# A four-layer graph network on one core: the first layer's first weight as seven half-size products between those of its third weight, and larger stated times for the eigenvectors' operations

## The chip, the cores and the metric

The kernel runs on one core of a Trainium2 chip. The metric is the device time of one execution in microseconds (us), as the median of several runs; the runs before are 2282.12, 2283.62 and 2285.63 us. The profile is of one further execution.

## What is computed

The reference is a chain of four graph layers on x of 128 x 64 x 256 numbers (64 nodes in each of 128 graphs, 256 features), all in float32, with a layer norm of the sum of input and output after each. Only the first layer, and what runs beside it, is touched:

```python
def layer0(x, adj, W1, W2, W3):           # W1 256x512, W2 512x1024, W3 1024x256
    def conv(x, W):
        return einsum('nm,bmh->bnh', adj * adj, einsum('bnf,fh->bnh', x, W))
    h = relu(conv(x, W1))
    h = relu(conv(h, W2))
    return conv(h, W3)
x = layernorm(x + layer0(x, adj, W1, W2, W3))
```

The second layer needs U, the eigenvectors of a 64 x 64 normalised Laplacian that is made from adj. It doesn't depend on x, so the kernel computes it beside the first layer. The second layer is relu(U^T x W1 + b1) W2 + b2, multiplied by U; the third has four small recurrences over windows; the fourth is attention.

## The kernel before, in words

**Groups and stages.** The 8192 rows of x form 64 tiles of 128 rows. The first layer takes them in 16 groups of 4 tiles (loop over `g` in `layer0`, L1136). For a group, `burst` (L1046) multiplies by the squared adjacency in 64 x 64 quadrants, from rows or from `h1`, and ScalarE copies the result from PSUM into `m1` or `m2` (L1058). `weigh` (L1111) multiplies `m1` by the first weight `aw1`: for each of 4 tiles two matmuls of 128x512, and a relu into `h1`. The second weight takes `m2` to `h2`, the third `h2` to `s3`, and `mix_rows` (L1116) multiplies by the adjacency once more and adds the input.

**Seven products.** The second and the third weight are computed as 2 x 2 block products by a scheme with seven products instead of eight (`seven`, L1079): sums of blocks of the weight are made once (`sums_of_weights`, L1026; `signed_sums`, L1032), sums of blocks of the data per group. For the second weight `sums_second` (L1129) makes these on VectorE. For the third they go into the tile `sh` by DMAs that add into their destination: `adds` (L1043) issues these from POOL's queue (L1044), and `less` (L1040) prepares negated blocks on ScalarE. Product 5 of the third weight reads slot 0 of `sh`, product 6 slot 1, product 7 slot 2 and product 3 slot 3. Products accumulate in PSUM banks: each chain holds one bank with the tag `ch` (two buffers), one `ps` (three buffers, shared with the bursts) and one `b5` (two buffers), by `bank` (L1023). Results are evicted by copies on ScalarE (L1096 to L1098), adds on VectorE, and where the result is an activation, a relu on ScalarE (L981) after the add.

**What sets the order.** This part of the kernel is scheduled by hand: the order of the Python code is the order on each engine. `seven` is a generator that emits one product at each step; `layer0` interleaves two chains for the second weight and then advances the chain `w3` of the third weight, with the four `weigh` between products 2 and 5 and the bursts for the next group between its later products. The eviction of a product is put off: `step` (L1014) emits the one before after the next product has been emitted.

**The eigenvectors beside it.** `eigen` (L275) is a generator, too: a Householder reduction of 62 steps, each with a 128x128 matmul into `pa` (L312), some 24 small VectorE operations and a square root on ScalarE (L397); then six passes of a bisection, a recurrence D2, and the vectors. `between` (L961), called after each matmul of the first layer, advances it when its time has come on a clock `now` that counts stated TensorE time. `Timed` (L42) wraps VectorE: each operation it emits moves the clock `free` on by a stated time `least` plus 0.0009 us for each element beyond 64. `V.least` is 0.21 us, in the bisection 0.278; `VL`, with 0.25, wraps the first layer's own VectorE operations. All operations through `Timed` carry L52 in the profile, all matmuls of the weights L972. The remaining layers are ordered by a planner (`Plan`) that the change doesn't touch; its instructions carry L162.

Of the kernel before, what the change touches and what calls it, by code (L numbers as in the profile page):

```python
# [11 lines left out]
F32 = mybir.dt.float32  # L12
# [29 lines left out]
class Timed:  # L42
# [1 line left out]


    def __init__(self, engine, free, until):
        self.engine, self.free, self.until, self.least = engine, free, until, 0.21

    def __getattr__(self, name):
        def give(out, *args, **kw):  # L50
# [224 lines left out]
def eigen(tc, stack, a, ident, cst, u2, ut2, now, free):  # L275
# [10 lines left out]
    until = [0.0]  # L286
    V, S, PE = Timed(nc.vector, free, until), nc.scalar, nc.tensor
# [5 lines left out]
    def sb(shape, tag):  # L293
        uid[0] += 1
        return wp.tile(shape, F32, tag=tag, name=f"{tag}_{uid[0]}")
# [9 lines left out]
    def soon():  # L305
        return max(free[0], until[0]) - 0.45
# [75 lines left out]
    for i in range(N - 2):  # L382
# [3 lines left out]
        q = sb([N, 16], "q")  # L386
# [67 lines left out]
    d, e, ep, g = (de[:, j:j + 1] for j in range(4))  # L454
# [40 lines left out]
    w = cp.tile([N, 20, N], F32, name="w")  # L495
# [66 lines left out]
    for _ in range(PASSES):  # L562
        V.tensor_scalar(h2, h2, 1.0 / (FAN + 1), None, op0=ALU.mult)
        x = sb([W, FAN], "bx")
# [4 lines left out]
        for k in range(1, HALF):  # L569
            r = sb([W, FAN], "br")  # L570
# [3 lines left out]
        r = sb([W, FAN], "br")  # L574
# [28 lines left out]
    for k in range(1, N):  # L603
        c = N - 1 - k
        t = sb([W, 1], "tw")
        V.reciprocal(t, D2[:, c + 1:c + 2])
        V.tensor_scalar(D2[:, c:c + 1], t, es2[:, k:k + 1], dl[:, k:k + 1], op0=ALU.mult, op1=ALU.add)
        yield soon()
    V.least = 0.21
    D = cp.tile([N, 2, N], F32, name="D")  # L610
    for k in range(2):
        V.tensor_scalar(D[:, k, :], D2[k * N:(k + 1) * N, :], 1e15, -1e15, op0=ALU.min, op1=ALU.max)
# [149 lines left out]
P = 128  # L762
# [74 lines left out]
def kernel(  # L837
# [26 lines left out]
    V, S, PE = nc.vector, nc.scalar, nc.tensor  # L864
# [14 lines left out]
    wa = phase_a.enter_context(tc.tile_pool(name="wa", bufs=1))  # L879
    pa = phase_a.enter_context(tc.tile_pool(name="pa", bufs=1))  # L880
# [3 lines left out]
    def load(pool, name, src, pattern, shape, **kw):  # L884
        t = pool.tile(shape, F32, name=name)
        nc.sync.dma_start(t, src.rearrange(pattern, **kw))
        return t
# [6 lines left out]
    order = list(range(RING, NT // 4)) + list(range(RING))  # L894

    def rows_of(g):

        return X[:, 4 * g:4 * g + 4, :] if g < RING else XA[:, 4 * (g - RING):4 * (g - RING) + 4, :]
# [11 lines left out]
    aw1 = load(wa, "aw1", a_w1, "(k p) f -> p k f", [P, 2, 512], p=P)  # L910
# [72 lines left out]
    def quads(c):  # L983
        for m in (slice(0, N), slice(N, P)):
            for h, hs in enumerate((slice(0, N), slice(N, P))):
                yield m, slice(c * P + m.start, c * P + m.stop), h, hs
# [5 lines left out]
    tv = wa.tile([P, 5, 4, P], F32, name="tv")  # L992
    m1 = pa.tile([P, 2, 512], F32, name="m1")
    h1 = pa.tile([P, 4, 512], F32, name="h1")
    m2 = pa.tile([P, 4, 512], F32, name="m2")
    ss = pa.tile([P, 3, 2, 256], F32, name="ss")
    h2 = pa.tile([P, 2, 8, 256], F32, name="h2")
    sh = pa.tile([P, 4, 4, 256], F32, name="sh")
    s3 = pa.tile([P, 4, D], F32, name="s3")
# [8 lines left out]
    free = [0.0]  # L1008
    VL = Timed(V, free, now)
# [13 lines left out]
    def bank(tag="ps"):  # L1023
        return tl(psa, [P, 512], tag, bufs={"ps": 3, "ch": 2, "b5": 2}[tag])

    def sums_of_weights(w, b12):  # L1026
        VL.tensor_sub(w[7], w[3], b12)
        VL.tensor_sub(w[5], b12, w[1])
        VL.tensor_sub(w[6], w[3], w[5])
        VL.tensor_sub(w[4], w[2], w[6])  # L1030

    def signed_sums():  # L1032
        w = third[0]
        VL.tensor_sub(w[7], D12, D22)
        VL.tensor_sub(w[5], D12, D11)
        VL.tensor_sub(w[6], D22, w[5])
        VL.tensor_sub(w[4], D21, w[6])
        VL.tensor_scalar(w[3], D22, -1.0, None, op0=ALU.mult)

    def less(slot, j, c):  # L1040
        S.activation(sh[:, slot, 2 * j:2 * j + 2], h2[:, 0, 4 * c + 2 * j:4 * c + 2 * j + 2, :], AF.Identity, scale=-1.0)

    def adds(out, src):  # L1043
        nc.gpsimd.dma_start(out, src, accum_op=ALU.add)  # L1044

    def burst(dst, src, c):  # L1046
        to = dst.rearrange("p c (t h n) -> p h c t n", h=2, n=N)
        p = [bank().rearrange("p (c t n) -> p c t n", c=2, t=4) for _ in range(2)]
        for t in range(4):
            for k in range(2):  # L1050
                for m, f, h, hs in quads(c + k):
                    PE.matmul(p[h][m, k, t, :], src[hs, t, f], sqT2[hs, hs], start=True, stop=True)  # L1052
        now[0] += QUADS
        between()

        def result():
            for h in range(2):
                S.copy(to[:, h, c:c + 2], p[h])  # L1058

        step(result)  # L1060

    def chained(out, pairs, new):
        for m, some in enumerate(pairs):
            for i, (lhsT, rhs) in enumerate(some):
                mm(out[:, m, :], lhsT, rhs, new and m == i == 0, i == len(some) - 1, skip_group_check=True)

    def by_second(j):

        def product(out, i, new):
            w, a = (x[i] for x in second)  # L1070
            chained(out, [[(w[:, k, c * P:(c + 1) * P], a[:, k, :]) for k in range(2)] for c in (2 * j, 2 * j + 1)], new)

        return product

    def by_third(out, i, new):
        w, a = (x[i] for x in third)
        chained(out, [[(a[:, k, r * P:(r + 1) * P], w[:, k, :]) for k in range(4)] for r in range(2)], new)

    def seven(n, product, c11, c12, c21, c22, last, order=(1, 2, 6, 5, 7, 3, 4)):  # L1079

        def view(b):
            return b[:, :2 * n].rearrange("p (i n) -> p i n", i=2)

        def add(dst, b):
            VL.tensor_add(dst, dst, b)
            if last is relu:
                relu(dst, dst)

        ch = view(bank("ch"))
        for i in order:  # L1090
            if i in (2, 5):
                b = view(bank("ps" if i == 2 else "b5"))
                b2, b5 = (b, None) if i == 2 else (b2, b)
            out = {2: b2 if i == 2 else None, 5: b5 if i == 5 else None, 3: b5 if i == 3 else None}.get(i, ch)
            product(out, i, i in (1, 2, 5))
            step({1: lambda: S.copy(c11, ch), 2: lambda: add(c11, b2), 6: lambda: S.copy(c12, ch),  # L1096
                  5: lambda: S.copy(c22, b5), 7: lambda: add(c22, ch), 3: lambda: add(c12, b5),
                  4: lambda: last(c21, ch)}[i])  # L1098
            yield i
# [11 lines left out]
    def weigh(t):  # L1111
        p = bank()
        run(p, [(m1[:, k, t * P:(t + 1) * P], aw1[:, k, :]) for k in range(2)])
        step(lambda: relu(h1[:, t, :], p))
# [21 lines left out]
    def layer0():  # L1136
        n = NT // 4
        burst(m1, rows_of(order[0]), 0)
        step()
        for t in range(4):  # L1140
            weigh(t)
            if t == 1:
                sums_of_weights(second[0], B12)
        step()
        for c in (0, 2):
            burst(m2, h1, c)
            step()
        for g in range(n):
            last = g == n - 1
            then = {} if last else {  # L1150
                (1, 1): lambda: less(2, 0, 0),
                (0, 5): lambda: (less(2, 1, 0), nc.sync.dma_start(sh[:, 1], sh[:, 2])),
                (1, 7): lambda: less(3, 0, 1),
                (0, 4): lambda: (nc.sync.dma_start(sh[:, 0], H22), adds(sh[:, 1], H22)),
                (1, 4): lambda: less(3, 1, 1),
            }
            sums_second()
            w2 = [seven(256, by_second(j), *[h2[:, r, 4 * c + 2 * j:4 * c + 2 * j + 2, :] for r in (0, 1) for c in (0, 1)],
                        relu) for j in range(2)]
            for j in (0, 0, 1, 0, 1, 0, 1, 0, 1, 0, 1, 0, 1, 1):  # L1160
                then.get((j, next(w2[j])), lambda: None)()
            if g == 0:
                signed_sums()
                burst(m1, rows_of(order[1]), 0)
            if last:
                for _ in plain():
                    pass
            else:
                q = [s3[:, r:r + 2, c:c + P] for r in (0, 2) for c in (0, P)]
                w3 = seven(P, by_third, *q, S.copy, order=(1, 2, 5, 6, 7, 3, 4))  # L1170
                next(w3)
                for slot in range(3):
                    adds(sh[:, slot], H21)
                adds(sh[:, 3], sh[:, 1])
                next(w3)
                for t in range(4):
                    weigh(t)
                next(w3)
                next(w3)
                burst(m2, h1, 0)  # L1180
                next(w3)
                next(w3)
                burst(m2, h1, 2)
                next(w3)
                if g + 2 < n:
                    burst(m1, rows_of(order[g + 2]), 0)
            for t in (0, 2):
                mix_rows(g, t)
        step()
# [71 lines left out]
    V, S, G, Q = (Noted(plan, e) for e in ("DVE", "ACT", "POOL", "SP"))  # L1261
# [585 lines left out]
```

## Time and profile before

| what | before |
|---|---|
| median of three runs | 2283.62 us |
| the profiled execution | 2283.95 us, its span 2282.0 us |
| first layer, from the start to the first matmul after it | 0 to 838.3 us |
| eigenvectors, last matmul | 689.6 us |
| TensorE matmul records, busy | 2236.5 us, 98% of the span |
| VectorE busy | 1710.0 us, 75% |
| ScalarE busy | 1217.1 us, 53% |
| granted TensorE clock | 0.995 |

The profile names the engines PE (TensorE matmuls), PEld (its weight loads), DVE (VectorE), ACT (ScalarE), POOL and SP. A line of the timeline gives the start, the length of the stretch, the engine, the source line, the operation with the tiles it writes and reads, the shape and how many records; a number in brackets is the engine's idle time just before, with what ended it. A float32 matmul leaves two records. Tiles are named without their numbers: `ps<-aw,m` is the first weight by `m1`, `ch<-aw,h` the first product of the third weight, `b<-tv,sh` its products 5 and 3, and `ps<-sqT,h` a burst. A line of busy times by stretch gives the stretch, its length, the busy time of each engine, the granted clock, the DMA engines' share and GB/s.

### The profile page before, as it was taken

What the parts mean: (1) busy time and instruction counts of PE and PEld (TensorE: products, weight loads), DVE (VectorE), ACT (ScalarE), POOL (GpSimd) and SP (SyncE); (2) the same over time, 40 slices, a digit from 0 to 9 for tenths busy, and PEclk for the clock granted to TensorE, in tenths of its full rate; (3) what the DMA queues carried; (4) which work ended last, traced back from release to release, by engine and by line L of the source; (5) the groups of instructions that cost most, each with busy time, mean ns of one, the idle gap of its engine ahead of it and who ended that gap; (6) DMA issues with size and microseconds to landing.
All of it is one profiled execution on the core that took longest, in us unless ns stands there. A gap on an engine that the chain in (4) does not pass through costs nothing.

```text
span 2282.0 us, 52665 instructions
## 1 busy us (share of the span) xinstructions
PE 2236.5 (98%) x20660; PEld 1993.6 (87%) x20660; DVE 1710.0 (75%) x5816; ACT 1217.1 (53%) x2954; POOL 204.1 (9%) x390
## 2 busy tenths in 40 slices
PE   7999999999999999999999999999999999999997
PEld 5877888888878888999999999999999999999985
DVE  5888888788881139766967977977877887578977
ACT  2444444454444445665655655655655656566554
POOL 0111111111111110000100000000010010000112
PEclk9999999999999999999999999999999999999998
DMA  8334333333443231000111211211221220001331
GB/s 267 74 89 90 87 77 75 75 82 77 108 93 79 66 125 57 11 10 20 66 38 50 77 57 50 86 57 40 87 66 40 78 72 32 31 29 64 110 115 49
DMA packets 95240, 163.01 MB, mean 71 GB/s; under 512 B 24976, under 2 KB 65936, under 8 KB 94992
## 3 DMA queue, kind: packets, MB, share of 16 engines
q1 hardware_dynamic: 83840, 120.05, 15.8%
q0 software_dynamic: 10800, 39.33, 9.1%
q8 instruction: 162, 2.65, 0.5%
q14 instruction: 86, 0.70, 0.1%
q10 hardware_dynamic: 352, 0.28, 0.0%
HBM read 57.64 MB, written 45.09 MB: 45 GB/s over the span
## 4 chain that ended last, share of the span: by engine, by line
PE 85%; DVE 10%; DMA 2%; issue 1%; ACT 1%; SPq 1%; POOL 1%; ACTq 0%; DVEq 0%; POOLq 0%
PE ps L162 57%; PE ch L972 12%; PE ps L972 9%; PE b L972 5%; PE ps L1052 2%; DVE q L52 1%; DVE w L162 1%; DMA XA<-in_x_dram 1%; DVE D L52 1%; DVE h L52 1%; DVE gates L162 1%; PE pa L312 1%; DVE X L162 1%; DVE xr L52 1%; DVE junk L52 1%
## 5 line engine op out<-in xcount | busy, mean ns | idle before, releaser
L162 PE MATMUL ps<-w,wih 128*128 128x128 f32 (+2 forms) x2944 | 572.0, 298 | 0.8 <-ACT gates L162 0.7
L162 PEld LDWEIGHTS ps<-w,wih 128*128 128x128 f32 x2944 | 453.1, 191 | 27.0 <-issue 6.5
L162 PE MATMUL ps<-w,sums 128*128 128x128 f32 (+2 forms) x3104 | 476.1, 293 | 0.0
L162 PEld LDWEIGHTS ps<-w,sums 128*128 128x128 f32 x3104 | 422.7, 191 | 13.9 <-ACT gates L162 1.6
L162 ACT ACTIVATE gates<-gates,cbi 128x256 f32<-128x256 f32 (+4 forms) x736 | 314.1, 479 | 172.0 <-DVE gates L162 170.1
L162 DVE TENSOR_TENSOR gates<-gates,ps 128x512 f32<-128x512 f32 (+4 forms) x408 | 233.9, 583 | 169.8 <-PE ps L162 156.8
L162 ACT COPY gates<-ps 128x512 f32<-128x512 f32 (+4 forms) x408 | 204.2, 506 | 252.0 <-PE ps L162 244.7
L162 PE MATMUL ps<-hs,whh 128*128 128x128 f32 (+1 forms) x896 | 181.2, 284 | 0.2 <-DVE hs L162 0.2
L162 PE MATMUL ps<-w,whh 128*128 128x128 f32 (+1 forms) x896 | 181.1, 284 | 0.0
L162 ACT ACTIVATE gates<-ps,cbi 128x128 f32<-128x128 f32 (+2 forms) x368 | 119.5, 385 | 43.3 <-PE ps L162 42.6
L162 POOL TENSOR_SCALAR rs<-mv 128x2 f32<-128x2 f32 x96 | 23.3, 253 | 1326.7 <-DVE mv L162 1325.4
L162 PEld LDWEIGHTS ps<-hs,whh 128*128 128x128 f32 x896 | 139.7, 191 | 0.3 <-DVE hs L162 0.3
L162 PEld LDWEIGHTS ps<-w,whh 128*128 128x128 f32 x896 | 139.8, 191 | 0.0
L981 ACT ACTIVATE h<-h 128x512 f32<-128x512 f32 x96 | 60.4, 630 | 147.7 <-DVE h L52 147.7
L972 PE MATMUL ch<-m,tw 128*128 128x256 f32 x512 | 123.3, 384 | 1.1 <-DVE h L52 0.8
L972 PE MATMUL ps<-aw,m 128*128 128x512 f32 x256 | 118.1, 607 | 1.2 <-ACT m L1058 1.2
L972 PE MATMUL b<-ss,aw 128*128 128x256 f32 x512 | 118.6, 379 | 0.0
L972 PEld LDWEIGHTS ch<-m,tw 128*128 128x128 f32 x512 | 96.7, 192 | 16.0 <-DVE h L52 3.5
L972 PEld LDWEIGHTS b<-ss,aw 128*128 128x128 f32 x512 | 97.2, 190 | 13.3
L972 PEld LDWEIGHTS ps<-aw,m 128*128 128x128 f32 x256 | 47.5, 194 | 50.8 <-issue 46.0
L162 PE MATMUL ps<-hs,sums 128*128 128x128 f32 (+1 forms) x448 | 90.6, 284 | 0.0
L162 ACT ACTIVATE gates<-c 128x256 f32<-128x256 f32 (+1 forms) x176 | 75.5, 432 | 27.4 <-DVE c L162 26.1
(369 smaller groups left out, 4150.4 us busy)
## 6 DMA issues: line engine op xcount, KB each, us to landing
sh<-h POOLq DMA_DIRECT2D x60, 512.0 KB, 6.5
far<-w SPq DMA_DIRECT2D x42, 512.0 KB, 2.8
w<-far SPq DMA_DIRECT2D x168, 128.0 KB, 3.0
X<-rest SPq DMA_DIRECT2D x24, 512.0 KB, 3.3
out_dram<-X SPq DMA_DIRECT2D x64, 128.0 KB, 1.8
sh<-sh SPq DMA_DIRECT2D x15, 512.0 KB, 2.9
sh<-h SPq DMA_DIRECT2D x15, 512.0 KB, 2.9
sh<-sh POOLq DMA_DIRECT2D x15, 512.0 KB, 4.9
```

The costliest lines, as they stand in the source:

```text
L52: return getattr(self.engine, name)(out, *args, **kw)
L162: getattr(e, name)(*[real(x) for x in args], **{k: real(v) for k, v in kw.items()})
L312: PE.matmul(out, lhsT, rhs, start=True, stop=True)
L972: PE.matmul(out, lhsT, rhs, start=start, stop=stop, **kw)
L981: S.activation(dst, src, AF.Relu)
L1052: PE.matmul(p[h][m, k, t, :], src[hs, t, f], sqT2[hs, hs], start=True, stop=True)
```

## The change

The first weight is made into seven products as well, from group 1 on (group 0 still uses `weigh`). A chain `w1` with a width of 256 is advanced between products of `w3`; its data sums are three VectorE operations on `m1` (`sums_first`), emitted while the group before its use is at the second weight, and a fourth (`X12`) after product 2. The order of the two chains' products is 3.1, 1.1, 3.2, 1.2, 1.6, 1.5, 3.5, 1.7, 1.3, 3.6, 1.4, where the digit before the point is the weight; then a burst for the upper half of `h1`'s columns, 3.7, a burst for the lower half, 3.3 and 3.4. Before, the lower half came first, after 3.6, and the upper after 3.3. The stated time of the eigenvectors' operations goes from 0.21 to 0.23 us; that of the bisection stays at 0.278.

```diff
-        self.engine, self.free, self.until, self.least = engine, free, until, 0.21
+        self.engine, self.free, self.until, self.least = engine, free, until, 0.23
...
-    V.least = 0.21
+    V.least = 0.23
...
+    W11, W12, W21, W22 = (aw1[:, r, c:c + 256] for r in (0, 1) for c in (0, 256))
+    tu = wa.tile([P, 3, 256], F32, name="tu")
+    X11, X12, X21, X22 = (m1[:, k, r:r + 256] for r in (0, 256) for k in (0, 1))
+    sx = pa.tile([P, 2, 256], F32, name="sx")
+    first = ((None, W11, W21, W22, tu[:, 2], W12, tu[:, 1], tu[:, 0]),
+             (None, X11, X12, X12, X22, sx[:, 0], sx[:, 1], X21))
...
+    def sums_first():
+        VL.tensor_add(sx[:, 0], X21, X22)
+        VL.tensor_sub(sx[:, 1], sx[:, 0], X11)
+        VL.tensor_sub(X21, X11, X21)
...
+    def by_first(out, i, new):
+        w, a = (x[i] for x in first)
+        chained(out, [[(a[:, r * P:(r + 1) * P], w)] for r in range(2)], new)
...
                 (1, 1): lambda: less(2, 0, 0),
+                (1, 6): lambda: sums_first() if g else None,
...
             if g == 0:
                 signed_sums()
+                sums_of_weights(first[0], W12)
                 burst(m1, rows_of(order[1]), 0)
...
-                q = [s3[:, r:r + 2, c:c + P] for r in (0, 2) for c in (0, P)]
-                w3 = seven(P, by_third, *q, S.copy, order=(1, 2, 5, 6, 7, 3, 4))
+                w3 = seven(P, by_third, *[s3[:, r:r + 2, c:c + P] for r in (0, 2) for c in (0, P)], S.copy,
+                           order=(1, 2, 5, 6, 7, 3, 4))
+                w1 = seven(256, by_first, *[h1[:, r:r + 2, c:c + 256] for r in (0, 2) for c in (0, 256)], relu)
                 next(w3)
                 for slot in range(3):
                     adds(sh[:, slot], H21)
                 adds(sh[:, 3], sh[:, 1])
+                if g == 0:
+                    sums_first()
+                next(w1)
                 next(w3)
-                for t in range(4):
-                    weigh(t)
-                next(w3)
+                next(w1)
+                VL.tensor_sub(X12, X12, sx[:, 1])
+                for w in (w1, w1, w3, w1, w1, w3, w1):
+                    next(w)
+                burst(m2, h1, 2)
                 next(w3)
                 burst(m2, h1, 0)
                 next(w3)
-                next(w3)
-                burst(m2, h1, 2)
                 next(w3)
```

## The prediction, made before the changed kernel had run

> **What bounds the kernel now.** I read the page's busy times first, then busy time by stretch, then TensorE's order of work in the stage that changes, then its waits, and last the engines that feed that stage.
>
> ```profile
> PE 2236.5 (98%) x20660; PEld 1993.6 (87%) x20660; DVE 1710.0 (75%) x5816; ACT 1217.1 (53%) x2954; POOL 204.1 (9%) x390
> ```
>
> TensorE bounds the whole. By stretch (PE, PEld, DVE, ACT, POOL busy us):
>
> ```profile
> 300.00:440.00 140.00, 139.63 (x1153) 114.24 (x1151) 114.62 (x651) 68.50 (x184) 19.73 (x33) 1.00 0.39 91
> 440.00:640.00 200.00, 200.00 (x1771) 166.38 (x1771) 174.58 (x651) 93.08 (x210) 27.28 (x44) 1.00 0.36 86
> 690.00:840.00 150.00, 149.50 (x1274) 125.74 (x1278) 29.14 (x49) 65.68 (x153) 16.26 (x30) 1.00 0.28 67
> ```
>
> Layer 0 lies at 0 to 838 us, and TensorE has hardly a gap in these stretches. VectorE is over 80% busy while the eigenvectors are computed (to 690 us), 19% after. A group without eigenvector work shows the stage that changes (start, length, records):
>
> ```profile
> 725.77 1.95 PE L972 MATMUL ch<-aw,h 128*128 128x128 f32 x16
> 727.55 1.95 PE L972 MATMUL ps<-aw,h 128*128 128x128 f32 x16
> 729.34 7.03 PE L972 MATMUL ps<-aw,m 128*128 128x512 f32 x16
> 736.21 1.95 PE L972 MATMUL b<-tv,sh 128*128 128x128 f32 x16
> ```
>
> From start to start, a product of the third weight takes 1.78 us and the first weight, plain, 6.87. Groups start every 49.12 us here (699.78, 748.90), every 51.7 to 53.1 in the Householder part. Where TensorE waits (in brackets):
>
> ```profile
> 47.45 0.46 PE L312 MATMUL pa<-AQ,LV 128*128 128x128 f32 x2 [3.44 <-DVE LV L52]
> 104.22 0.46 PE L312 MATMUL pa<-AQ,LV 128*128 128x128 f32 x2 [0.74 <-DVE LV L52]
> 161.81 1.99 PE L972 MATMUL ch<-m,tw 128*128 128x256 f32 x8 [0.35 <-DVE h L52]
> 643.56 2.05 PE L972 MATMUL ch<-tv,h 128*128 128x128 f32 x16 [0.93 <-DVE s L52]
> ```
>
> All such waits from 60 to 690 us come to 6.2 us: VectorE behind its stated times. Last, what stands behind a group's final products (third weight begins at 320.46 there):
>
> ```profile
> 320.93 0.67 DVE L52 TENSOR_TENSOR h<-h,b 128x512 f32<-128x512 f32 x1
> ```
>
> ```profile
> 321.63 0.63 ACT L981 ACTIVATE h<-h 128x512 f32<-128x512 f32 x1 [0.83 <-DVE h L52]
> 322.29 0.63 ACT L1041 ACTIVATE sh<-h 128x512 f32<-128x512 f32 x1
> 322.83 0.58 ACT L981 ACTIVATE h<-ch 128x512 f32<-128x512 f32 x1
> ```
>
> ```profile
> 319.69 0.92 POOL L1044 DMA_DIRECT2D sh<-h  x1 [4.56 <-ACT h L981]
> 323.77 0.86 POOL L1044 DMA_DIRECT2D sh<-h  x1 [3.17 <-ACT LV L385]
> ```
>
> The second weight's last add starts 0.47 us after the third's first product, and ScalarE reads the `ch` bank of its last product until 323.4, 2.95 us after it. In the group at 725.77 the same read ends 0.97 us after. Nobody needed this bank or these sums soon; the change makes two products need them.
>
> **What the Trainium skill says.** "Perfetto Trace Analysis", Identifying the Most-Contended Engine: matmul busy share is no measure of distance from the limit; look at weight loads. The trace agrees: matmul records overlap (379 ns long, 216 apart), so I price by starts. Same page, Matmuls: independent groups should rotate through PSUM banks, so that eviction overlaps; with two `ch` banks for four chains this is where I expect the cost. "VectorE: DVE Perf Modes", the TRN2 errata: an fp32 tensor_tensor takes (N+151)/0.96 ns, so 424 ns for 256 and 691 for 512 elements; the trace has 410 (`s<-s,ps`) and 674 (`h<-h,b`). "DMA: Bandwidth & Descriptors", Anatomy of one DMA: 2.0 us plus bytes at 436 GB/s, an estimate of 3.2 us for 512 KB; the accumulating ones here land after 4.6 (727.11) to 6.5 us (375.59), and I use these.
>
> **The change, part by part.** I call the start of the third weight's first product 0, its products 3.1 to 3.7, the first weight's 1.1 to 1.7.
>
> *TensorE work.* Removed in each of groups 0 to 14: 6.87 us. Added: 7 products of 2 matmuls, 4 records of 128x256 each; eight such records take 1.73 us (751 to 765), so 28 take 6.04. Saved 0.83 x 15 = **12.4 us**, on the path, since TensorE is busy throughout there.
>
> *VectorE and ScalarE work.* Per group VectorE gets four 128x256 operations (0.41) and three 128x512 adds (0.67): 3.7 us in 48, some 8%; it had 18% free. ScalarE had four evictions (2.4 us), now three copies, three relus and one eviction (4.2): hidden, it is half idle. `sums_first` stands seven products before it is needed. Group 0 pays 1.6 us of weight sums behind a backlog on VectorE; product 1.6 starts at 5.3, the sums are done some 3 us in: nothing, or 1 us if late. The 8% itself I cost at nothing, covered by the free share; with that gone it would be 3.7 us a group.
>
> *Stated times 0.21 to 0.23.* VectorE's real pitch is 0.212 (24 operations of a Householder step in 5.09 us from 329.33), more in early groups. With 0.23 it keeps pace, so most waits above go: of 2.4 us before `LV` some 1.7, of the 0.84 before `h` all, of the 3.44 at 47.45 about 1: **-3.5 us** (0 to -5). The eigenvectors end later: in the built order their last matmul moves into group 15, with 60 half-products of 0.43 us and 1.7 us behind it, 27 us. So the end stays covered; without that cover each us of delay counts in full.
>
> *Wait A: 1.1 for its bank.* It takes the bank of the second weight's last product, and stands at 1.78. ScalarE frees it 2.5 us after the last add starts. Following the built order of VectorE, ScalarE and the eigenvector matmuls, with these durations, over its five repeating phases the add starts at about -0.4, 0, -0.8, 0.2 and 0.7, which makes waits of 0.4, 0.7, 0, 0.9 and 1.2. Ten groups (0 to 9) have Householder steps, so 6.4; I take **5.9 us** (3 to 10), as later steps have shorter operations. In the groups with the bisection the POOL issue came at 1.34 to 2.0, hence the bank at 1.0 to 1.6: no wait.
>
> *Wait B: the burst right after 1.4.* It reads what 1.3 completes, through an add (0.67) and a relu (0.63), with 3.6 and 1.4 (2.64 us) as cover. In the same five phases 0, 0.3, 1.0, 0.5, 0, over nine groups: **3.2 us** (1 to 6). Queued behind the waiting matmuls is all of TensorE's order, including eigenvector matmuls.
>
> *Wait C: 3.5 for the accumulating DMA.* It moves from 10.4 (736.21) to 7.0. The DMA's issue at 1.34 lands at 5.9 without eigenvector work; in the other groups at 3.3, landing at 8.7 (323.77 and 5.4). Wait A itself delays 3.5 to 7.9 on average, with an eigenvector matmul 8.2. What remains: **1 us** (0 to 15). The later accumulates (3.6, 3.7, 3.3) have over 1 us to spare. POOL's and SP's queues keep their order; nothing passes them.
>
> *Group 14* now meets the D2 recurrence, where two operations take 0.505 us against a stated 0.46: 1 us (0 to 3).
>
> *After layer 0* the built order of TensorE is unchanged; only release waits of the later weights' loads differ, on tiles finished earlier: nothing. A load freed 1 us late could cost that 1 us; there is no gain in it, since the loads issued at 821 to 839 us land before VectorE's first sums of them (850.8).
>
> **Sum** against the profiled execution (2283.95 us, span 2282.0 and 1.95 around it): -12.4 - 3.5 + 5.9 + 3.2 + 1 + 1 = -4.8, so 2279.1. The median of the runs is 0.33 us lower: **2278.7**.
>
> **Rivals.** 0.2% (4.6 us) is about what a measurement can tell from no change.
> 1. *The waits hardly come.* A slower stated pace lets VectorE run ahead to its data, as in the bisection groups; A and B fall to some 2 us and C and group 14 to none: -12.4 - 3.5 + 2 = -13.9, 2269.7. For: bisection groups show no such delay. Against: the constant 3.3 us issue in five groups, set by ScalarE's square root in between.
> 2. *The waits take all.* A and B at their upper ends (16 us): -12.4 - 3.5 + 16 + 2 = +2, 2286; or, in the middle, 2283. For: both waits hang on three engines' queues in a row.
> 3. *Slower: C decides.* In the group at 372.21 the add was issued at 3.4 and landed at 9.9, 2.6 us after 3.5 would want it. If half of the ten groups are so, C is 13, A in the rest 3.5, B 3.2, group 14 1: -15.9 + 20.7 = +4.8, 2288.4. It decides once landings in the ten groups average beyond some 9.3. For: H22's add is in the same queue. Against: in the built order that add comes earlier.
>
> **Chances.** Forecast (gain of 3 to 9 us) 0.45, rival 1 0.20, rival 2 0.22, rival 3 0.13. Beyond 0.2% faster: rival 1 and 0.27 of the forecast, 0.47; slower: rival 3 and 0.02 of rival 2, 0.15; the rest, 0.38, the same. Range: 2270.5, leaving out a quarter of rival 1, to 2288.5, leaving out half of rival 3.
>
> **What would show it.** The first weight's 28 records in 6.0 us; groups 10 to 13 at about 48.3 us; waits before `ch<-aw,m` (A) near 0.6 us a group and before `ps<-sqT,h` (B) near 0.3, up to about 480 us; no wait on a DMA before `b<-tv,sh`. The forecast is wrong if C stands there regularly, if bisection groups wait too, or if the eigenvectors end after layer 0.

## The result and the profile after

The changed kernel takes 2281.1 us (median of 20 runs), the kernel before 2284.77 in the same comparison: a ratio of 0.9983, 95% interval 0.9976 to 0.9990, so 3.9 us faster (2.3 to 5.5). The profiled execution took 2280.57 us with a span of 2278.8; before, the span was 2282.0. The first matmul after the first layer starts at 834.10 (before 838.34), 4.2 us earlier. What follows takes 1444.7 us, before 1443.7; over the profiles of both kernels and of experiments 1 to 11 it scatters from 1442.0 to 1444.7, so that 1.0 us is not read as an effect. One place alone makes up more than that: four records of a later matmul, `ps<-w,dw`, take 3.65 us from 2186.02 at a granted clock of 0.79 (2184 to 2192), behind a wait of 2.43 us; before, they take 1.96 us at 1.00, behind a wait of 2.33 us.

Busy times of the whole, first part of the page after:

```profile
PE 2224.0 (98%) x20840; PEld 2026.2 (89%) x20840; DVE 1758.0 (77%) x5925; ACT 1239.0 (54%) x2999; POOL 205.2 (9%) x390
```

TensorE's busy time fell by 12.5 us, the span by 3.2. The difference, 9.3 us, is idle time of TensorE that was not there before. Busy time by stretch shows it (PE, PEld, DVE, ACT, POOL):

```profile
300.00:440.00 140.00, 137.37 (x1325) 122.54 (x1324) 110.17 (x575) 70.58 (x187) 18.62 (x30) 1.00 0.39 91
440.00:640.00 200.00, 198.04 (x1821) 174.83 (x1820) 162.35 (x681) 100.02 (x239) 26.60 (x44) 1.00 0.36 85
690.00:840.00 150.00, 145.21 (x1185) 125.40 (x1185) 103.30 (x387) 67.75 (x161) 17.60 (x33) 1.00 0.30 78
```

PE is idle for 2.6, 2.0 and 4.8 us in these stretches, where it was for 0.4, 0 and 0.5. VectorE's 103 us in the last stretch (before 29) are the eigenvectors, which now reach into groups 14 and 15; their last matmul is at 806.04, 28 us ahead of the end of the layer. The stage that changed, in a group where nothing waits here (start, length, records, the timeline of PE):

```profile
616.55 1.95 PE L972 MATMUL ch<-aw,h 128*128 128x128 f32 x16
618.33 1.03 PE L972 MATMUL ch<-aw,m 128*128 128x256 f32 x4
619.20 1.95 PE L972 MATMUL ps<-aw,h 128*128 128x128 f32 x16
620.98 1.03 PE L972 MATMUL ps<-aw,m 128*128 128x256 f32 x4
621.85 1.03 PE L972 MATMUL ch<-tu,sx 128*128 128x256 f32 x4
```

A product of the first weight takes 0.87 us from start to start (618.33 to 619.20, 620.98 to 621.85), seven of them 6.1 instead of 6.87. Group 11 is 48.76 us long (590.55 to 639.31), 0.38 of it a wait. The waits, from the timeline of PE (idle time before, with its releaser, in brackets):

```profile
49.36 0.77 PE L312 MATMUL pa<-AQ,LV 128*128 128x128 f32 x2 [4.33 <-DVE LV L52]
...
110.49 1.13 PE L972 MATMUL ch<-aw,m 128*128 128x256 f32 x4 [0.70 <-ACT h L981]
123.56 1.16 PE L1063 MATMUL ps<-sqT,h 64*64 64x64 f32 x64 [0.91 <-ACT h L981]
...
264.45 1.13 PE L972 MATMUL ch<-aw,m 128*128 128x256 f32 x4 [1.02 <-ACT h L981]
...
630.28 1.16 PE L1063 MATMUL ps<-sqT,h 64*64 64x64 f32 x64 [0.38 <-ACT h L981]
673.74 2.02 PE L972 MATMUL b<-tv,sh 128*128 128x128 f32 x16 [1.25 <-DMA sh<-h]
...
762.88 1.99 PE L972 MATMUL ch<-m,tw 128*128 128x256 f32 x8 [0.51 <-DVE h L52]
768.19 1.13 PE L972 MATMUL ch<-aw,m 128*128 128x256 f32 x4 [1.53 <-ACT h L981]
...
789.90 1.95 PE L972 MATMUL ps<-s,sqT 128*128 128x512 f32 x4 [1.08 <-DVE s L52]
```

`ch<-aw,m` behind ScalarE is wait A (product 1.1 for its bank), `ps<-sqT,h` wait B (the burst for the relu of 1.3), `b<-tv,sh` behind a DMA wait C. A comes in groups 1 to 7 and 9 with 0.70, 0.92, 0, 1.02, 0.93, 0.32 and 0.61, and 0.70; group 3 and, five groups on, group 8 have none: it repeats every five groups, and shrinks. These eight groups come to 5.2 us. B comes seven times with 0.22 to 0.91. Waits on `LV` are gone but for the first one, which has grown from 3.44 to 4.33. The last three lines shown, 3.1 us together, lie in group 14 and are counted there: D2's operations stand on VectorE from 724.1 to 764.2, so the first wait falls beside them and the other two behind them. The 1.53 is of A's kind; with it A is 6.7 us.

How A comes about, in group 1. VectorE:

```profile
107.85 0.69 DVE L52 TENSOR_TENSOR h<-h,b 128x512 f32<-128x512 f32 x1
```

and ScalarE:

```profile
108.57 0.63 ACT L981 ACTIVATE h<-h 128x512 f32<-128x512 f32 x1 [1.92 <-DVE h L52]
109.23 0.63 ACT L1052 ACTIVATE sh<-h 128x512 f32<-128x512 f32 x1
109.77 0.19 ACT L397 ACTIVATE q<-q 64x1 f32<-64x1 f32 x1
109.86 0.57 ACT L981 ACTIVATE h<-ch 128x512 f32<-128x512 f32 x1
```

The bank is read by the last line, which ends at 110.43; 1.1 starts at 110.49. Ahead of this relu stand the relu of the sum that VectorE made (108.57) and a negation for `sh` (`less`, L1052), which nobody needs yet at this point. Experiment 9 starts from here.

### The profile page after: what moved, and what is told of

It is laid out like the page before. It is cut to its first block, busy times and chain, and to the rows that moved or that the text cites. A ratio compares the mean times of both kernels' runs of the same rounds, so it can differ in the third digit from the quotient of the medians.

```text
span 2278.8 us, 53192 instructions
## 1 busy us (share of the span) xinstructions
PE 2224.0 (98%) x20840; PEld 2026.2 (89%) x20840; DVE 1758.0 (77%) x5925; ACT 1239.0 (54%) x2999; POOL 205.2 (9%) x390
## 4 chain that ended last, share of the span: by engine, by line
PE 83%; DVE 10%; DMA 2%; ACT 2%; issue 1%; SPq 1%; POOL 0%; ACTq 0%; DVEq 0%; POOLq 0%
PE ps L162 57%; PE ch L972 12%; PE b L972 6%; PE ps L972 5%; PE ps L1063 2%; DVE h L52 1%; DVE w L162 1%; DMA XA<-in_x_dram 1%; ACT h L981 1%; DVE D L52 1%; PE pa L312 1%; DVE X L162 1%; DVE gates L162 1%; DVE q L52 1%; DMA sh<-h 1%
## 5 line engine op out<-in xcount | busy, mean ns | idle before, releaser
L981 ACT ACTIVATE h<-h 128x512 f32<-128x512 f32 x141 | 89.0, 631 | 248.3 <-DVE h L52 248.2
L162 DVE TENSOR_TENSOR w<-w,w 128x128 f32<-128x128 f32 (+2 forms) x264 | 80.7, 316 | 8.1 <-PE ps L162 4.4
L162 DVE SCALAR_TENSOR_TENSOR c<-gates,c 128x256 f32<-128x256 f32 (+1 forms) x112 | 50.0, 446 | 41.1 <-ACT gates L162 40.8
```

The lines of the kernel that those rows point to most:

```text
L162: getattr(e, name)(*[real(x) for x in args], **{k: real(v) for k, v in kw.items()})
L981: S.activation(dst, src, AF.Relu)
```

## The experiments

The theory: the products save what they should, and the eigenvectors' small operations, in the order of VectorE and ScalarE, delay what 1.1, 3.5 and the burst wait for. The rivals: the products lose by themselves (banks, DMAs), and the stated time is what gains, or the other way round. All times are against the kernel before, run beside each kernel; the yardstick of the changed kernel is its 0.9983. A difference between two such ratios is uncertain by some 3 us (an estimate from the intervals of both). Against the changed kernel, experiments 1, 6 and 7 are slower and 10 and 11 faster beyond this; 5, 8, 9 and 12 lie about as far from it as this or nearer, so there the single waits in the traces carry the argument.

C counts every wait of 3.5 that ends within 0.15 us of the landing of its DMA. The profile puts some of these down to a VectorE instruction (`b<-tv,sh` at 321.89 in experiment 5, landing at 321.76).

**1. The seven products alone, with the old stated time.**

```diff
-        self.engine, self.free, self.until, self.least = engine, free, until, 0.23
+        self.engine, self.free, self.until, self.least = engine, free, until, 0.21
...
-    V.least = 0.23
+    V.least = 0.21
```

> The seven products alone, with the stated time left at 0.21. Theory (the seven products save 12.4 us of TensorE work and pay in waits for evictions that stand behind eigenvector operations on VectorE; the larger stated time takes VectorE out of arrears): the saving stays, the old waits before LV and h stay and the new ones grow, so 3 to 7 us slower than the changed kernel, about level with the kernel before. Rival (the larger stated time only moves the eigenvectors' end and buys nothing): level with the changed kernel, 4 us faster than before.

Measured: 2289.8 us against 2283.62, ratio 1.0029 (1.0018 to 1.0039): 6.2 us slower than before, some 10 slower than the changed kernel, more than expected. Two of its waits on PE:

```profile
113.97 1.13 PE L972 MATMUL ch<-aw,m 128*128 128x256 f32 x4 [2.60 <-ACT h L981]
...
161.69 0.46 PE L312 MATMUL pa<-AQ,LV 128*128 128x128 f32 x2 [0.72 <-DVE LV L52]
```

A adds up to 11.9 us (6.7 in the changed kernel with group 14), the waits on `LV` after the first to 2.5 (none), C to 2.3, B to 4.0, about what it was in the changed kernel. The layer ends at 844.77. So the seven products on their own lose. The reading that VectorE has more of the first layer's work, and is told to take the eigenvectors' operations faster than it can, fits these waits.

**2. The stated time alone**, in the kernel before.

```diff
-        self.engine, self.free, self.until, self.least = engine, free, until, 0.21
+        self.engine, self.free, self.until, self.least = engine, free, until, 0.23
...
-    V.least = 0.21
+    V.least = 0.23
```

> The kernel before with only the stated time of the eigenvectors' operations raised to 0.23, no seven products for the first weight. Theory: some of the 6.2 us of waits from 60 to 690 us go, 2 to 4 us faster than before. Rival (the whole gain of the change is the seven products' net): within 1 us of before.

Measured: 2282.46 against 2283.62, ratio 0.9993 (0.9985 to 1.0001): by the ratio 1.6 us, which the interval can't tell from nothing. The waits before `LV` that remain are 0.17 to 0.33, but the wait of 3.4 that was 0.93 is 2.71, one group later:

```profile
688.30 1.65 PE L972 MATMUL ch<-tv,h 128*128 128x128 f32 x6 [2.71 <-DVE s L52]
```

The product starts 6.5 us behind the end of D2 (681.8), whose own stated time the change leaves at 0.21 (L602). It also costs more than its length: behind it the granted clock is 0.57 from 688 to 696, and what then stands up to 696.52 takes 8.2 us, where the same work before (643.56 to 648.46) takes 4.9; only 0.25 of the difference is a small matmul that stands between. So 0.23 alone might gain more with D2's time fitted; no run here tried it. As run, neither part gives the 3.9 us alone, and together they do. That the slower pace makes room on VectorE for the products' operations is the reading; experiment 1 against the changed kernel, some 10 us, is what shows that the products need it.

**3 and 4. Both kernels without the eigenvectors.** These two leave the eigenvectors out and give the second layer zeros in their place.

```diff
-    eig.extend([0.0, eigen(tc, phase_a, adst[:N, :], ident, eig_c, u2, ut2, now, free)])
...
+        V.memset(u2, 0.0)
+        V.memset(ut2, 0.0)
```

> The kernel before without the eigenvectors: they are left out and set to zero, so the second layer works on zeros. Base for the next run. First layer groups at 49.1 us, with the burst of the next rows, all along; some 20 to 35 us faster than before, since the eigenvectors' matmuls (about 0.3 us for each of 63 steps) and the waits go.

> The changed kernel without the eigenvectors (left out and set to zero). Theory (waits A, B and C come from eigenvector operations in front of the evictions): no wait before the first weight's first product nor before the burst, so the full 12.4 us faster than the kernel before without eigenvectors (11 to 13). Rival (the waits come from the seven products' own evictions on ScalarE and VectorE): waits remain and the difference is 4 to 8 us.

Measured: 2245.64 (ratio 0.9835, 0.9822 to 0.9849) and 2235.83 (0.9791, 0.9778 to 0.9805), so 9.8 us between them; their layers end at 800.77 and 790.83, 9.9 apart. Groups take 49.12 and 48.30 us. In the second no product or burst waits for a relu, not even 0.15 us: A and B come from the eigenvectors' operations alone. The expected 11 to 13 us were missed by what the following lines show (PE, with the products and without the eigenvectors):

```profile
51.79 1.13 PE L972 MATMUL ch<-aw,m 128*128 128x256 f32 x4 [1.24 <-ACT m L1069]
...
638.55 2.02 PE L972 MATMUL b<-tv,sh 128*128 128x128 f32 x16 [0.50 <-DMA sh<-h]
```

In group 0, 1.1 waits 1.24 us for a burst's copy, so that group gains 0.42 instead of 0.83 (from its 3.1 to the next); and C comes three times, 1.05 us in all, so C does not come from the eigenvectors alone.

**5. 1.1 one product later**, behind 3.2, so that its bank has 1.78 us more; the order of the first weight's products becomes that of the third's.

```diff
-                w1 = seven(256, by_first, *[h1[:, r:r + 2, c:c + 256] for r in (0, 2) for c in (0, 256)], relu)
+                w1 = seven(256, by_first, *[h1[:, r:r + 2, c:c + 256] for r in (0, 2) for c in (0, 256)], relu,
+                           order=(1, 2, 5, 6, 7, 3, 4))
...
-                next(w1)
                 next(w3)
                 next(w1)
+                next(w1)
```

> The changed kernel with the first weight's first product moved behind the third weight's second one (order 3.1, 3.2, 1.1, 1.2, 1.5, 1.6, 3.5 and on), so that its bank is wanted 1.8 us later. Theory: wait A (6.7 us listed in the changed kernel) falls below 1.5, but product 3.5, which stays at the same place and was delayed by A, now meets the accumulating DMA: wait C grows from 1.3 to 3 to 8. Net -5 to +2 us against the changed kernel. Rival (A is a cost of its own): C stays near 1.3 and the kernel is 5 to 6 us faster than the changed one, 9 to 10 faster than before.

Measured: 2278.19 against 2283.93, ratio 0.9971 (0.9960 to 0.9983), 5.7 us faster than before and, by the ratios, 2.7 better than the changed kernel, as its theory expected. A is gone, 6.7 us; but C, once 1.25 us, is now 5.7 in seven groups. All waits of PE from 40 us to the end of the layer fall from 18.6 to 16.7 us. POOL's issue and the wait of 3.5, in the timelines of POOL and of PE (3.1 begins at 261.99):

```profile
265.27 0.85 POOL L1055 DMA_DIRECT2D sh<-h  x1 [3.82 <-ACT s L1111]
```

```profile
271.26 0.94 PE L972 MATMUL b<-tv,sh 128*128 128x128 f32 x6 [1.86 <-DMA sh<-h]
```

The DMA is issued 3.3 us after 3.1 and lands 5.9 later, 9.2 after 3.1. In the changed kernel the issue in this group is at 264.76, it lands at 270.17, and 3.5 starts at 270.21 without a wait, because A and the products between have held it back. A had paid for C.

**6 and 7. The burst one product later**, after 3.7, to take away B; alone, and with the move of experiment 5.

```diff
+                next(w3)
                 burst(m2, h1, 2)
-                next(w3)
                 burst(m2, h1, 0)
```

> The changed kernel with the third weight's product 7 ahead of the burst for the upper columns, which gives the add and the relu behind product 1.3 another 1.8 us. Theory: wait B (4.1 us listed) goes, 3 to 4 us faster than the changed kernel. Rival (the work just moves its wait): product 3.7 waits for the copy of 3.6 out of its bank, which now has 0.9 us, and the time stays within 1.5 us of the changed kernel.

> Both moves: 1.1 behind 3.2, and 3.7 ahead of the burst. Theory: the sum of the two runs above, against the changed kernel -8 to -1 us. Rival (A and B hide one another, since a TensorE that waits at A lets VectorE gain on it): removing both gives less than the better one alone plus 1 us.

Measured: 2292.83 (ratio 1.0034, 1.0022 to 1.0047) and 2288.37 (1.0020, 1.0012 to 1.0028): 8.9 and 4.4 us slower than before. Experiment 6 on PE:

```profile
126.16 2.05 PE L972 MATMUL ch<-tv,sh 128*128 128x128 f32 x16 [1.31 <-ACT s L1111]
...
129.99 1.15 PE L1063 MATMUL ps<-sqT,h 64*64 64x64 f32 x62 [0.59 <-ACT m L1069]
```

B is gone, as it should be, and two waits stand in its place. Its rival had named the second of them, but not its size; the first I had not foreseen. The two bursts now follow each other, each fills two `ps` banks, and there are three: the second waits 0.59 us for a copy in 13 groups, 7.7 us. And 3.7, which B had held back, now waits for a `ch` bank until ScalarE has copied 3.6 out of it, behind the same relu: eight waits, 6.8 us. In experiment 7 the same two stand with 7.7 and 7.2 us, and C with 6.0, so it too fails its theory of 1 to 8 us faster than the changed kernel. The theory for B holds (what was waited for), the cure doesn't.

**8. D2's stated time from 0.21 to 0.255** (L602), about half of the 0.505 us that a pair takes.

```diff
-    V.least = 0.21
+    V.least = 0.255
```

> The changed kernel with the stated time of the D2 recurrence, which the change left at 0.21, raised to 0.255 (two operations take 0.505 us). Theory: the waits of group 14 (3.1 us between 760 and 792 us) fall to under 1, 2 to 2.5 us faster than the changed kernel; the eigenvectors end some 6 us later, still 20 us before the layer does. Rival (those waits come from the vector part after D2): they stay, no change.

Measured: 2276.78, ratio 0.9969 (0.9956 to 0.9981), 7.2 us faster than before and, by the ratios, 3.2 better than the changed kernel. The waits agree: of the three in group 14, 3.1 us, the first two are gone, but for 0.21 before 3.5, and the third is smaller:

```profile
786.60 1.95 PE L972 MATMUL ps<-s,sqT 128*128 128x512 f32 x4 [0.75 <-DVE w L52]
```

**9 to 11. The negation behind the relu.** `less(3, 1, 1)`, which stood ahead of the relu in the ScalarE lines above, is emitted after 3.1; then the same with the edit of 8, then with those of 8 and 5.

```diff
-                (1, 4): lambda: less(3, 1, 1),
...
                 next(w3)
+                less(3, 1, 1)
```

> The changed kernel with one ScalarE operation (the last negated block, 0.6 us, which is needed only by product 3.3) emitted after the relu that frees the bank, instead of ahead of it. Theory (A is the chain add, relu, negation, relu ahead of the bank, and the same chain starts the DMA): each wait before 1.1 falls by 0.55 to 0.65 us, their sum from 6.7 to 2 to 3, and wait C doesn't grow, since the DMA is issued earlier by the same amount: 3.5 to 5 us faster than the changed kernel. Rival (the DMA's own landing sets the pace): C takes back over half of it.

> The run above with the D2 recurrence's stated time at 0.255 as well. Theory: the two are apart in time, so they add up: 2 to 2.5 us faster than the run above, some 10 us faster than before. Rival: no more than the better of the two.

> The run above with the first weight's first product behind the third weight's second one as well. Theory: wait A goes to zero, and C, with the DMA issued 0.6 us earlier, stays under 3 us: 0 to 2 us faster than the run above. Rival (C is bound by the queue of accumulates): C near 5 us again, level or slower.

Measured, against 2285.22: 2277.79 (ratio 0.9973, 0.9962 to 0.9984), 2275.05 (0.9960, 0.9948 to 0.9972) and 2275.25 (0.9959, 0.9947 to 0.9971). ScalarE in the first, group 1 again:

```profile
108.29 0.63 ACT L981 ACTIVATE h<-h 128x512 f32<-128x512 f32 x1 [1.93 <-DVE h L52]
108.83 0.19 ACT L397 ACTIVATE q<-q 64x1 f32<-64x1 f32 x1
108.92 0.57 ACT L981 ACTIVATE h<-ch 128x512 f32<-128x512 f32 x1
109.40 0.62 ACT L1052 ACTIVATE sh<-h 128x512 f32<-128x512 f32 x1
```

The relu follows its predecessor at once, and the wait of 0.70 in this group is gone. A falls from 6.7 to 1.7 us over the layer (0.25 to 0.36 in three groups, 0.87 in group 14), but C rises from 1.25 to 3.4, as in 5, so that the layer ends 2.9 us earlier and the ratio gains 2.3, less than the 3.5 to 5 expected. With D2's time the layer ends at 828.26, 5.8 us earlier than the changed kernel's: 2.9 of each, the two add up (counted from the end of the first wait on `LV`, whose length scatters, 2.4 and 2.6 of 5.0). By the ratio this is 9.1 us (6.4 to 11.9) faster than before, level with experiment 11 as the fastest. Moving 1.1 as well brings nothing more: C is 4.3, nearer to its rival's 5 than to the theory's 3, and the layer ends later, at 831.40. What follows takes 1442.0 instead of 1444.2 us; most of this is the place named under the result, where the granted clock is 0.79 in experiment 10 (2178 to 2186) and 1.00 in 11 (2180 to 2188).

**12. 0.25 in place of 0.23**, so that the eigenvectors end after the layer.

```diff
-        self.engine, self.free, self.until, self.least = engine, free, until, 0.23
+        self.engine, self.free, self.until, self.least = engine, free, until, 0.25
...
-    V.least = 0.23
+    V.least = 0.25
```

> The changed kernel with the stated time at 0.25 instead of 0.23. In the built order the last eigenvector matmul then stands 2 us behind the first layer's last matmuls, so the cover is gone. Theory: waits A and B fall a little further (1 to 2 us), and the end of the eigenvectors stands bare, with the transposes at their end each waiting on VectorE: 3 to 10 us slower than the changed kernel. Rival (a slower stated pace goes on paying): 1 to 3 us faster than the changed kernel.

Measured: 2279.23, ratio 0.9972 (0.9962 to 0.9983), by the ratio 6.4 us faster than before. I had expected it to lose 3 to 10 us against the changed kernel; it is level with it or slightly ahead, which is its rival. The uncovered end is there, on PE:

```profile
829.60 0.44 PE L312 MATMUL pa<-AQ,Z 64*64 64x64 f32 x2 [2.20 <-DVE junk L52]
830.86 0.48 PE L312 MATMUL pa<-ident,UT 64*64 64x64 f32 x4 [0.82 <-DVE UT L52]
```

With 0.56 and 0.31 behind these it waits 3.9 us, and the part from 826.91 to the end takes 6.2 us more than in the changed kernel (1450.9 against 1444.7). But 826.91 is 7.2 us earlier than 834.10: the slower pace takes most of A (2.2 us are left) and B (1.7), and of group 14's 3.1 us 0.96 is left at the same place. C, at 4.3, has grown here too. The waits explain 3.9 of the 6.2. Behind them the granted clock is 0.66 from 828 to 838 (1.00 in the changed kernel from 800 to 850), and the matmuls `ps<-u,X` take 3.71 us where the changed kernel takes 2.09; that is 1.6 more.

## Why the prediction was right

The time predicted was 2278.7 us, measured 2281.1; faster, near the 0.2% that a measurement can tell. The mechanism was right: the products save what was forecast, and new waits on evictions behind the eigenvectors' operations take most of it back. That the sum comes so close is in part luck: old waits and A fell out 2.0 us better than forecast, B, C and group 14 3.2 worse. By the terms of the sum, in us; what is measured is read from the two profiles:

| term | predicted | measured |
|---|---|---|
| TensorE work | -12.4 | -12.5 (PE busy) |
| old waits | -3.5 | -4.8 |
| A | +5.9 | +5.2 |
| B | +3.2 | +4.1 |
| C | +1 | +1.25 |
| group 14 | +1 | +3.1 |
| after the layer | 0 | +1.0, within the scatter |
| span | -4.8 | -3.2 (the terms: -2.7) |

*TensorE work* was priced right, by starts and not by lengths of records. Experiments 3 and 4 give 0.82 us a group by itself. That group 0 might pay for its weight sums was named; what it waits for in experiment 4 was another thing, the copies of a burst.

*Old waits.* Those listed before came to 6.2 us; 0.56 of them stays, all others from 60 us on are gone. The first, at 47.45, was to fall by about 1 and rose by 0.9. No fall is shown, and the rise can't be read as an effect: over the changed kernel and experiments 5 to 11, which don't differ ahead of it, this wait scatters from 3.07 to 5.23 us (with 0.21 it is 3.44 and, in experiment 1, 3.68).

*A.* The cause (experiment 4), the place and the pattern of five groups were right: for 0.4, 0.7, 0, 0.9 and 1.2 in five phases, groups 1 to 5 show 0.70, 0.92, 0, 1.02 and 0.93. The runs add what the prediction hadn't: up to 0.63 us of each of these waits is a negation that merely stands ahead.

*B* was right in cause. In the groups for which it was sized it comes to 3.24 us, as forecast, but not in the forecast phases, so the sum is partly luck: for 0, 0.3, 1.0, 0.5 and 0, groups 1 to 5 show 0.91, 0, 0.89, 0 and 0. The rest is groups 11 and 13, with 0.38 and 0.47, for which the sum had nothing; that bisection groups wait was one of the prediction's own signs of being wrong. Groups 10 to 13 take 48.6 to 49.8 us from 3.1 to 3.1, not the 48.3 named there. In group 11 VectorE has

```profile
627.98 1.07 DVE L52 SCALAR_TENSOR_TENSOR M<-Q,in 128x512 f32<-128x512 f32 x1
628.88 0.68 DVE L52 TENSOR_TENSOR h<-h,b 128x512 f32<-128x512 f32 x1
```

ahead of the relu that the burst needs. The prediction took the bisection's groups as undisturbed from one place in the order (POOL's issue); its 128x512 operation falls elsewhere. In group 13 (728.91) D2 had begun.

*C* came once, with 1.25 us, but its size was met by luck. It was sized for the ten groups of the Householder part, which have none; the one wait stands in group 12, beside the bisection, where the sum had none. There the DMA was issued at 667.04, 1.7 us after 3.1, and landed 6.6 later. In the ten groups it landed 7.5 us after 3.1 on average, at most 8.7; the prediction had taken 8.7 for most. Rival 3 was to decide once these landings average beyond some 9.3: they average 7.5 in experiment 5 too, with one at 9.2, so its own mark was not near. That A holds 3.5 back was in the prediction's step for C, and experiment 5 shows it: without A, C is 5.7 us. So A is not a cost that can be had back by itself; taking it away left 1.9 us less waiting in all.

*Group 14* is the term mis-sized most, 3.1 instead of 1, and from a misreading: the step set D2's 0.505 us against "a stated 0.46", but the change leaves D2 at 0.21 (as the list of stated times ahead of the prediction should have said), so 0.42 for the pair. Over D2's 63 pairs VectorE then falls some 5 us behind (an estimate from these times). Experiment 8, with 0.255, takes the first two waits away, 2.0 us. The third is another thing: VectorE itself stands idle for 3.71 us before it, until a matmul of the eigenvectors ends (788.86), and experiment 8 leaves 0.75 of it.

*The end's cover* was 28 us, as forecast (27). "Without that cover each us of delay counts in full" is what experiment 12 puts in question: the uncovered end cost 6.2 us, but the layer before it ended 7.2 earlier.

*Rivals 1 and 2.* The waits didn't fall to 2 us: experiment 4 shows what rival 1 would need, no eigenvector work at all. With 0.21, in experiment 1, rival 2 is what happens, and more so.

## What to carry to other kernels

A saving on the bounding engine that splits work into shorter products can bring waits on evictions that nobody had waited for; price them by following each eviction through the order of its engine, and look for an instruction ahead of it that could stand behind it (here 0.63 us of negation; moved, the layer ends 2.9 us earlier). Of waits that follow each other on one engine, the first pays for part of the next: take one away and see what the next becomes (6.7 us of A gone, 4.5 us of C come). Where work is interleaved by stated times, check for each of its parts that the stated pace is the real one, and re-tune it whenever the first stream changes: 0.23 in place of 0.21 gained 1.6 us in the old order, not clear of nothing, and some 10 in the new.

## What the runs showed of the hardware that was not expected

Two bursts in a row, each filling two of three banks, cost the second one 0.59 us each time in experiment 6, about the length of the one copy that has to free a bank (128x512, 0.59 us; the one at 129.35 ends at 129.94, and the burst starts at 129.99). The Trainium skill, "Perfetto Trace Analysis", Matmuls, asks that independent groups rotate through banks; this trace puts a number on a rotation that is one bank short. The accumulating DMAs of 512 KB took longer than I had priced, with 4.6 and 6.5 us from two of them: over all 75 it is 4.5 to 9.0 us, median 5.7, in the changed kernel, and 4.5 to 9.4, median 6.0, before. In group 12 of the changed kernel two of them, issued one right after the other at 670.10, landed after 6.0 and 7.9 us, and the one that 3.5 waits for (667.04) after 6.6. From 664 to 677 the core's DMA engines are over 90% busy there, at 235 GB/s on average. That these transfers wait for one another is the likely reading, not shown by an experiment.

A wait of TensorE can cost more than its length. After the wait of 2.71 us in experiment 2 and that of 2.20 in experiment 12 the granted clock falls, to 0.57 over 8 us and 0.66 over 10. But after 2.60 us in experiment 1 (113.97) it stays at 1.00, and of the nearly equal waits late in both kernels, 2.33 and 2.43 us, only the second is followed by a fall, to 0.79 over 8 us. The length of the wait doesn't decide it by itself here, and what does stays open. In this case the falls move the time by 1.6 to 3 us each, as much as the effects that are being compared.
